# One scan instruction for two states, and lane X's second half moved ahead of scan and exponentials

## The chip, the cores and the metric

The kernel runs on one core of a Trainium2 chip. The core has five instruction streams: TensorE (PE, matmuls; PEld is its weight load), VectorE (DVE), ScalarE (ACT), GpSimd (POOL) and SyncE (SP), which issues nearly all DMA transfers here. Each stream runs in its own order and waits on semaphores where it needs another stream's result. The metric is the device time of one execution in microseconds, and lower is better.

## The reference

The input is `x` of shape (4, 128, 64, 64): 4 images of 128 channels and 4096 pixels. The layers are:

```
x = x + conv_mamba(group_norm(x))          # layer 0
t = tokens(x)                              # (4, 4096, 128)
t = t + attention(layer_norm(t))           # 4 heads of 32, 4096 x 4096 scores
t = t + top2_experts(layer_norm(t))        # 8 experts
```

Inside layer 0 the normalised image goes through a 3x3 depthwise convolution and is cut into four groups of 32 channels. For each group a state-space recurrence runs over the 4096 pixels, with 64 inner channels and 16 states for each of them:

```
dA  = exp(delta * A)               # per inner channel, state, pixel
dBu = delta * B * xin
h   = dA * h + dBu                 # one step per pixel, 16 states side by side
y   = sum over states of h * C
```

`delta`, `B` and `C` depend on the pixel. `B` and `C` are shared by all the inner channels of a group. After that come a gate, a projection, a norm and another projection.

## The kernel before

The pixels of an image are cut into 8 blocks of 512 columns. Two groups of channels with 64 inner channels each fill the 128 partitions, so a block has two parts (`p`) and each part has 16 states (`n`). A *unit* is one state of one part of one block: 4 images x 8 blocks x 2 parts x 16 states = 1024 units. The main loop (line 1244) takes one unit per pass, and a pass is called a *slot*. For its unit a slot issues:

- on SP, one 512 KB load `rows` with `B` and `C` of one state, for the unit three slots later (`fetched`, line 732);
- on ACT, the exponential `da` for the unit two slots later (`decayed`), and a copy of the last column of the previous unit's `h` into `state`, which the next block of the image starts from (line 1253);
- on DVE, three instructions (`scan`, line 747): `h = B * du`, the scan `h`, and `hc = h * C`;
- on PE one slot later, the sum over states: `hc` is added into the PSUM tile `y`. In the first 128 slots (`ALONE`) this is a matmul with the identity. Later it is four transposes of 128 columns (`turned_on`), whose sum is copied to `yT` on ACT after the part's last state and is transposed back a slot later (`turned_back`). DVE then forms `xin` from `y`. There is one `y` buffer.

In the same slot one *group* of attention work is issued (line 1257). A group has two tiles of 128 keys: four score matmuls `sc` on PE, two exponentials `pT` of 128x1024 on ACT, and in the next slot eight products with the values, `av`, on PE (`weighted`). All images together have 1024 groups. Attention for an image starts when its first three blocks are finished, so it lags behind the recurrence and goes on after the last unit. `sc` has two PSUM buffers, so the scores of a slot need the exponentials of the slot before.

All other work is written as generators that stop at each `yield`, and runs in two lanes. Lane Y holds the norms, the convolution and the `inputs` of the recurrence. Lane X holds `closed` (what follows the recurrence up to queries, keys and values) and `finished` (what follows attention, with the experts). `advance(lane, second)` runs one stage. A lane takes one stage in its first half and one in its second half of a slot. A task starts in a first half and ends in one. In lane X all PE work stands in first halves, at the end of a slot, and nearly all DVE and ACT work, which reads its results, stands in second halves.

Nothing reorders this: `Queue` (line 439) chains every instruction of an engine to the one issued before it, so the order of the Python calls is the order of every engine's queue. In a slot that order is:

```
sends; rows load; state copy; da; sc and pT; h, scan, hc; X second half; Y first half;
turned_back; y; Y second half; av; X first half
```

All recorded instructions of the main loop carry line 445, that of the `Queue` helper, so the profile's groups are told apart by their tiles.

## Time and profile before

| | |
|---|---|
| median of 3 runs | 5479.84 us (5469.26 to 5483.6) |
| the profiled execution | 5476.1 us, its span 5474.3 us |
| mean granted TensorE clock | 0.96 |
| PE busy | 4898.3 us (89% of the span) |
| DVE busy | 4126.6 us (75%) |
| ACT busy | 3928.8 us (72%) |
| POOL busy | 1249.9 us (23%) |
| DMA | 1131.83 MB, mean 207 GB/s |

The span starts with the first instruction and ends with the last one. A group of the profile is one kind of instruction on one set of tiles: its row gives the count, the busy time, the mean length of one, and how long its engine had stood idle just before, with what ended that idle time. `out<-in` names the tile written and the tiles read. A median beside a mean shows whether the mean is made by a few long ones. PE's own waits are the best sign of what holds it, since PE is the busiest engine. The table of windows gives each engine's busy time in a stretch of the span.

### The profile page before, as it was taken

The numbers are of one execution on the slowest core, as the hardware profiler recorded it, in microseconds if no ns is written. First come the engines' busy times: TensorE is split into PE (matmuls) and PEld (weight loads), VectorE is DVE, ScalarE is ACT, GpSimd is POOL, SyncE is SP. The second block draws the span as 40 slices with busy tenths as digits, with TensorE's granted clock in tenths as the row PEclk, the third lists the DMA queues.
The fourth block names the chain that finished last, engine by engine and source line by source line (L and its number), as shares of the span: only waits on it lengthen the run. The fifth ranks groups of instructions, "written<-read, shape, count | busy, mean of one in ns | idle before, by whom it ended". The sixth has DMA issues, their size and how long they took to land.

```text
span 5474.3 us, 66026 instructions
## 1 busy us (share of the span) xinstructions
PE 4898.3 (89%) x20778; PEld 2337.6 (43%) x20778; DVE 4126.6 (75%) x6659; ACT 3928.8 (72%) x6045; POOL 1249.9 (23%) x1085
## 2 busy tenths in 40 slices
PE   4677898999999998999999998999999999999997
PEld 2223344444444444444444444444444444444443
DVE  4988778888778888888888888888888888761231
ACT  3555677888777787787877787777777777765553
POOL 2222223223312223223312213222221222200100
PEclk8778999999999999999999999999999999999998
DMA  3556567667666667666766666667766666655442
GB/s 97 175 176 197 190 204 242 224 225 245 218 208 209 222 215 245 221 219 225 257 211 213 213 222 227 231 199 243 253 203 207 205 227 216 234 198 170 166 148 69
DMA packets 451719, 1131.83 MB, mean 207 GB/s; under 512 B 51985, under 2 KB 135330, under 8 KB 451362
## 3 DMA queue, kind: packets, MB, share of 16 engines
q1 hardware_dynamic: 450194, 1126.74, 61.3%
q8 instruction: 167, 2.74, 0.2%
q14 instruction: 190, 1.56, 0.1%
q10 hardware_dynamic: 1168, 0.80, 0.1%
HBM read 967.12 MB, written 143.39 MB: 203 GB/s over the span
## 4 chain that ended last, share of the span: by engine, by line
PE 54%; DVE 19%; ACT 12%; DMA 7%; issue 6%; SPq 1%; POOL 0%; DVEq 0%; ACTq 0%; POOLq 0%
PE av L445 20%; PE sc L445 13%; PE ps_X L445 9%; DVE h L445 9%; PE ps_Y L445 6%; PE y L445 5%; ACT pT L445 4%; ACT xt L445 3%; DMA ks<-kd 2%; ACT L445 2%; DVE hc L445 2%; DMA rows<-bcd 1%; DMA inv<-inverse 1%; DVE share L445 1%; DVE cm L445 1%
## 5 line engine op out<-in xcount | busy, mean ns | idle before, releaser
L445 ACT ACTIVATE pT<-sc 128x1024 f32<-128x1024 f32 x2048 | 1983.7, 1022 | 965.4 <-PE sc L445 962.5
L445 PE MATMUL av<-pT,v 128*64 128x512 f32 x8192 | 1996.9, 608 | 3.8 <-ACT avs L445 3.6
L445 PE MATMUL sc<-qs,ks 128*128 128x512 f32 x4096 | 1302.9, 439 | 99.3 <-DMA ks<-kd 51.4
L445 DVE TENSOR_TENSOR_SCAN h<-da,state,h 128x512 f32<-128x512 f32 x896 | 1240.7, 1385 | 108.5 <-ACT da L445 14.8
L445 PEld LDWEIGHTS sc<-qs,ks 128*128 128x128 f32 x4096 | 715.1, 192 | 773.2 <-ACT pT L445 236.4
L445 DVE TENSOR_TENSOR h<-rows,du 128x512 f32<-128x512 f32 x1024 | 826.3, 807 | 75.1 <-ACT state L445 38.0
L445 DVE TENSOR_TENSOR hc<-rows,h 128x512 f32<-128x512 f32 x1024 | 826.2, 807 | 51.5 <-PE sc L445 0.5
L445 PEld LDWEIGHTS av<-pT,v 128*64 128x64 f32 x8192 | 499.9, 137 | 813.1 <-issue 784.8
L445 ACT ACTIVATE da<-delta,amat 128x512 f32<-128x512 f32 x1024 | 750.5, 733 | 11.1 <-DVE h L445 7.0
L445 PE MATMUL y<-ident,hc 128*128 128x128 f32 x3584 | 555.8, 279 | 57.2 <-DVE xin L445 46.9
L445 PEld LDWEIGHTS y<-ident,hc 128*128 128x128 f32 x3584 | 443.0, 143 | 242.3 <-issue 90.4
L445 ACT ACT_TABLE_LOAD x319 | 409.3, 1283 | 19.3 <-PE ps_Y L445 14.1
L445 POOL TENSOR_TENSOR rsX<-rsX,mhalf 128x4 f32<-128x4 f32 x92 | 114.2, 1241 | 1031.9 <-DVE shiftX L445 1031.9
L445 POOL TENSOR_TENSOR rsY<-rsY,mhalf 128x4 f32<-128x4 f32 x100 | 141.0, 1410 | 826.3 <-DVE shiftY L445 825.5
L445 ACT COPY state<-h 128x1 f32<-128x1 f32 x896 | 176.7, 197 | 191.2 <-DVE h L445 190.7
L445 POOL TENSOR_TENSOR zs<-xin,zs 128x512 f32<-128x512 f32 x64 | 107.4, 1678 | 871.2 <-DVE xin L445 871.2
L445 POOL TENSOR_TENSOR avs<-avs,prev 128x512 f32<-128x512 f32 x96 | 139.3, 1451 | 719.0 <-ACT avs L445 402.7
L445 POOL TENSOR_SCALAR du<-e 128x512 f32<-128x512 f32 x64 | 126.2, 1972 | 578.7 <-ACT e L445 578.7
L445 DVE TENSOR_TENSOR share<-share,xf 128x1024 f32<-128x1024 f32 x128 | 172.6, 1348 | 109.6 <-DMA share<-sharesX 75.3
L445 PE MATMUL ps_X<-share,w_ew 128*128 128x512 f32 x432 | 215.6, 622 | 23.2 <-DVE share L445 23.2
L445 PE MATMUL y<-hc,ident 128*128 128x512 f32 x256 | 169.1, 758 | 42.4 <-DVE hc L445 42.2
L445 DVE TENSOR_TENSOR res<-res,ps_X 128x512 f32<-128x512 f32 x108 | 73.9, 685 | 154.4 <-PE ps_X L445 153.6
(238 smaller groups left out, 4566.2 us busy)
## 6 DMA issues: line engine op xcount, KB each, us to landing
rows<-bcd SPq DMA_DIRECT2D x1024, 512.0 KB
ks<-kd SPq DMA_DIRECT2D x192, 512.0 KB
qs<-qd SPq DMA_DIRECT2D x161, 512.0 KB
share<-sharesX SPq DMA_DIRECT2D x108, 512.0 KB
v<-vd SPq DMA_DIRECT2D x192, 256.0 KB
ks<-kd SPq DMA_DIRECT2D x128, 256.0 KB
avd<-avs SPq DMA_DIRECT2D x96, 256.0 KB
prev<-avd SPq DMA_DIRECT2D x96, 256.0 KB
```

What stands on the lines that cost most here:

```text
L445: return lambda *args, **kw: queued(op(*args, **kw))
```

## The change

A unit now covers two neighbouring states, `n` and `n + 1`, and takes two slots, so the number of slots for the recurrence stays 1024.

- **Layout.** A `rows` load now brings `B` of both states or `C` of both states. It is still 1024 values for each of the 128 partitions, and there is still one load per slot. The host orders the weight `wbc` so that the stored `B` and `C` lie this way.
- **DVE.** In the even slot one multiply of 1024 columns forms both `h` inputs (`driven`), and one scan runs over 1025 columns. Between the two states lies a column whose `da` is zero and whose input is the second state's starting value, so the scan restarts there. In the odd slot one multiply of 1024 columns forms both `hc` (`read`).
- **ACT.** `da` is written one state per slot into one of two fixed tiles, for the next unit. A copy puts the second state's starting value into its column (`carried`). One copy per unit keeps the last columns of both states (`kept`), at the end of the even slot.
- **Order.** Lane X's second half is issued ahead of the attention group and the scan. In the even slot it stands behind `driven`; in the odd slot it stands ahead of `read`. The exponentials are split from the score matmuls (`exponentials`) and follow lane X's second half.
- **Sum over states.** The transposes (`turned_on`, `turned_back`) are used from the start. The two terms are due one and two slots after the odd slot. The first term of a part is due one slot later than that after the first half image (`late`).
- **Buffers.** `h` has 2 of 1026 columns (3 of 512 before), `hc` has 2 of 1024 (5 of 512 before), lane X's `tmp` has 6 (4 before), and `hi` and `lo` of the queries and keys now come from it.

The loop's new text and the helpers are below. The rest of `closed` and the host's ordering of `wbc` are left out.

```diff
--- before.py
+++ after.py
@@ -488,7 +488,9 @@
         return ps_work.tile(shape or [P, BLK], F32, tag=f"work{lane}", name=f"ps_{lane}")
 
     def tmp(lane, name, shape=None):
-        return side.tile(shape or [P, BLK], F32, tag=f"tmp{lane}", name=name, bufs=4)
+        return side.tile(
+            shape or [P, BLK], F32, tag=f"tmp{lane}", name=name, bufs=6 if lane == "X" else 4
+        )
 
     def transposed(lane, src):
         ps = work(lane)
@@ -703,8 +705,8 @@
         held.clear()
         bc = tmp("Y", "bc")[0:DI, :]
         scalar.copy(bc, pb[0:DI, :])
-        bcd = dram.tile([2, NST, 2 * BLK], F32, name="bcd", bufs=4)
-        send(bcd.rearrange("c n (k q) -> (c n k) q", k=2), bc)
+        bcd = dram.tile([2, NST // 2, 2, 2 * BLK], F32, name="bcd", bufs=4)
+        send(bcd.rearrange("c n k (m q) -> (c n k m) q", m=2), bc)
 
         e = tmp("Y", "e")
         scalar.activation(e, ps, AF.Abs, bias=dtb)
@@ -728,34 +730,58 @@
         yield
 
     states = [mix.tile([P, 2, NST], F32, name=f"state{k}") for k in range(2)]
-
-    def fetched(b, i, p, n):
-
-        bcd = in_of[b, i, p][4]
+    decays = [mix.tile([P, 2, BLK + 1], F32, name=f"da{k}") for k in range(2)]
+    for k in range(2):
+        gpsimd.memset(decays[k][:, 0, BLK:], 0.0)
+
+    def fetched(unit, k):
+
+        b, i, p, n = unit
         w = mix.tile([P, 2, BLK], F32, name="rows", bufs=4)
         sync.dma_start(
-            out=w.rearrange("p k q -> p (k q)"),
-            in_=bcd[:, n, :][None].to_broadcast([DI, 2, 2 * BLK]),
+            out=w.rearrange("p m q -> p (m q)"),
+            in_=in_of[b, i, p][4][:, n // 2, k, :][None].to_broadcast([DI, 2, 2 * BLK]),
         )
         return w
 
-    def decayed(b, i, p, n):
-        da = mix.tile([P, BLK], F32, name="da", bufs=3)
-        scalar.activation(da, in_of[b, i, p][2], AF.Exp, scale=amat[:, n : n + 1])
-        return da
-
-    def scan(b, i, p, n, w, da):
-
+    def decayed(unit, da, k):
+        b, i, p, n = unit
+        scalar.activation(
+            da[:, k, 0:BLK], in_of[b, i, p][2], AF.Exp, scale=amat[:, n + k : n + k + 1]
+        )
+
+    def carried(unit):
+
+        b, i, p, n = unit
+        if (i, p, n) == (0, 0, 0):
+            gpsimd.memset(states[b % 2], 0.0)
+        h = mix.tile([P, 2, BLK + 1], F32, name="h", bufs=2)
+        scalar.copy(h[:, 0, BLK:], states[b % 2][:, p, n + 1 : n + 2])
+        return h
+
+    def kept(unit, h):
+        b, i, p, n = unit
+        if i < NB - 1:
+            scalar.copy(states[b % 2][:, p, n : n + 2], h[:, :, BLK - 1])
+
+    def driven(unit, h, w):
+        b, i, p, n = unit
         du = in_of[b, i, p][3]
-        h = mix.tile([P, BLK], F32, name="h", bufs=3)
-        vector.tensor_mul(h, w[:, 0, :], du)
+        vector.tensor_mul(h[:, :, 0:BLK], w, du[:, None, :].to_broadcast([P, 2, BLK]))
+
+    def scan(unit, h, da):
+
+        b, i, p, n = unit
+        h, da = (a.rearrange("p k q -> p (k q)")[:, 0 : 2 * BLK + 1] for a in (h, da))
         vector.tensor_tensor_scan(
-            out=h, data0=da, data1=h, initial=0.0 if i == 0 else states[b % 2][:, p, n : n + 1],
+            out=h, data0=da, data1=h, initial=states[b % 2][:, p, n : n + 1],
             op0=ALU.mult, op1=ALU.add,
         )
-        hc = mix.tile([P, BLK], F32, name="hc", bufs=5)
-        vector.tensor_mul(hc, w[:, 1, :], h)
-        return h, hc
+
+    def read(h, w):
+        hc = mix.tile([P, 2, BLK], F32, name="hc", bufs=2)
+        vector.tensor_mul(hc, w, h[:, :, 0:BLK])
+        return hc
 
     def scanned(b, i, p, y):
         xin, zs, delta, du, bcd = in_of.pop((b, i, p))
...
@@ -961,7 +983,7 @@
                     nxt = parts[at + 1]
                     if ready(b, nxt):
                         ahead = load(nxt, qs if nxt[:2] == (q, h) and not nxt[5] else None)
-                pTs = []
+                scs = []
                 for j in range(g, g + STEP):
                     sc = ps_sc.tile([P, 2, BLK], F32, name="sc")
                     for u in range(2):
@@ -969,14 +991,20 @@
                             sc[:, u, :], ks[:, j * P : (j + 1) * P],
                             qs[:, u * BLK : (u + 1) * BLK],
                         )
-                    pT = att.tile([P, 2, BLK], F32, name="pT", bufs=4)
-                    scalar.activation(pT, sc, AF.Exp, scale=ATT_SCALE)
-                    pTs.append((v[:, j // NT, j % NT, :], pT))
+                    scs.append((v[:, j // NT, j % NT, :], sc))
                 yield (
-                    b, q, h, pTs, first and g == 0, last and g + STEP == NT * n, prev, final,
+                    b, q, h, scs, first and g == 0, last and g + STEP == NT * n, prev, final,
                 )
 
     sums, partial, total, inverse, later = [None], {}, {}, {}, deque()
+
+    def exponentials(group):
+        pTs = []
+        for v, sc in group[3]:
+            pT = att.tile([P, 2, BLK], F32, name="pT", bufs=4)
+            scalar.activation(pT, sc, AF.Exp, scale=ATT_SCALE)
+            pTs.append((v, pT))
+        return *group[:3], pTs, *group[4:]
 
     def weighted(group):
         b, q, h, pTs, first, last, prev, final = group
@@ -1162,12 +1190,12 @@
         while True:
             if lane not in running:
 
-                tasks = lanes[lane] if lanes[lane] or slot < len(units) else lanes["X"]
+                tasks = lanes[lane] if lanes[lane] or slot < END else lanes["X"]
                 if not tasks or not all(k in done for k in tasks[0][2]):
                     return False
 
                 if (
-                    tasks[0][0][0] == "out" and slot < len(units) + 4
+                    tasks[0][0][0] == "out" and slot < END + 4
                     and not 2 <= slot % (2 * NST) < NST + 2
                 ):
                     return False
@@ -1236,53 +1264,70 @@
         left.clear()
 
     groups = attention_groups()
-    units = [(b, i, p, n) for b, i in blocks for p in range(2) for n in range(NST)]
-
-    ALONE = NB // 2 * 2 * NST
-    rows, decays, old, due, closing = {}, {}, None, deque(), deque()
-    y_of, waiting, slot = {}, None, 0
-    while slot < len(units) or due or closing or waiting or left or later or lanes["X"] or running:
+    units = [(b, i, p, n) for b, i in blocks for p in range(2) for n in range(0, NST, 2)]
+    END = 2 * len(units)
+
+    ALONE = NB // 2 * NST
+    rows, due, closing, y_of = {}, deque(), deque(), {}
+    h_of, slot = {}, 0
+
+    def fetch(*wanted):
+        for ahead, k in wanted:
+            if ahead < len(units):
+                until(("in", *units[ahead][:3]))
+                rows[ahead, k] = fetched(units[ahead], k)
+
+    def prepared(ahead, k):
+        if ahead < len(units):
+            decayed(units[ahead], decays[ahead % 2], k)
+            if k:
+                h_of[ahead] = carried(units[ahead])
+
+    def ends(unit):
+        return unit[3] == NST - 2
+
+    waiting = None
+
+    while slot < END or due or closing or waiting or left or later or lanes["X"] or running:
+        at, odd = divmod(slot, 2)
         flush()
-
-        for ahead in range(slot if slot == 0 else slot + 3, min(slot + 4, len(units))):
-            until(("in", *units[ahead][:3]))
-            rows[ahead] = fetched(*units[ahead])
-        if old:
-            (b, i, p, n), h = old
-            if i < NB - 1:
-                scalar.copy(states[b % 2][:, p, n : n + 1], h[:, BLK - 1 : BLK])
-            old = None
-        for ahead in range(slot if slot == 0 else slot + 2, min(slot + 3, len(units))):
-            decays[ahead] = decayed(*units[ahead])
+        if slot == 0:
+            fetch((0, 0), (0, 1), (1, 0))
+            prepared(0, 0)
+            prepared(0, 1)
+        fetch((at + 2, 0) if odd else (at + 1, 1))
+        unit = units[at] if at < len(units) else None
+        prepared(at + 1, odd)
+        if unit and not odd:
+            h = h_of.pop(at)
+            driven(unit, h, rows.pop((at, 0)))
+        advance("X", True)
         group = next(groups, None)
-        if slot < len(units):
-            unit = units[slot]
-            h, hc = scan(*unit, rows.pop(slot), decays.pop(slot))
-            old = unit, h
-            b, i, p, n = unit
-
-            due.append((slot + 1, unit, hc, n == 0))
-        advance("X", True)
+        if group:
+            group = exponentials(group)
+        if unit and not odd:
+            scan(unit, h, decays[at % 2])
+        if unit and odd:
+            hc = read(h, rows.pop((at, 1)))
+            late = slot >= ALONE and unit[3] == 0
+            due.append((slot + 1 + late, unit, 0, hc[:, 0, :], False))
+            due.append((slot + 2, unit, 1, hc[:, 1, :], ends(unit)))
         advance("Y", False)
         while closing and closing[0][0] <= slot:
             turned_back(*closing.popleft()[1:])
         while due and due[0][0] <= slot:
-            at, unit, term, first = due.popleft()
-            b, i, p, n = unit
+            _, (b, i, p, n), k, term, done_with = due.popleft()
+            first = n == 0 and k == 0
             if first:
                 y_of[b, i, p] = ps_y.tile([P, BLK], F32, name="y")
-            y, ends = y_of[b, i, p], n == NST - 1
-            if at <= ALONE:
-                mm(y, ident, term, first, ends)
-                if ends:
-                    summed_up(b, i, p, y_of.pop((b, i, p)))
-            else:
-                turned_on(y, term, first, ends)
-                if ends:
-                    yT = mix.tile([P, BLK], F32, name="yT")
-                    scalar.copy(yT, y_of.pop((b, i, p)))
-                    closing.append((slot + 1, b, i, p, yT))
+            turned_on(y_of[b, i, p], term, first, done_with)
+            if done_with:
+                yT = mix.tile([P, BLK], F32, name="yT")
+                scalar.copy(yT, y_of.pop((b, i, p)))
+                closing.append((slot + 1, b, i, p, yT))
         advance("Y", True)
+        if unit and not odd:
+            kept(unit, h)
         if waiting:
             weighted(waiting)
         waiting = group
...
```

More of the change, by code (lines that the diff above doesn't have):

```diff
@@ L852, in closed @@
             yield
-            hi = side.tile([P, BLK], F32R, name="hi", bufs=2)
-            vector.tensor_scalar(hi, ps, bias, None, ALU.add)
-            lo = side.tile([P, BLK], F32R, name="lo", bufs=2)
-            vector.scalar_tensor_tensor(
-                lo, ps, bias, hi.bitcast(F32), ALU.add, ALU.subtract
-            )
+            hi, lo = tmp("X", "hi"), tmp("X", "lo")
+            vector.tensor_scalar(hi.bitcast(F32R), ps, bias, None, ALU.add)
+            vector.scalar_tensor_tensor(lo.bitcast(F32R), ps, bias, hi, ALU.add, ALU.subtract)
             for half, w in enumerate((hi, lo)):
-                w = w.bitcast(F32)
                 if len(d.shape) == 4:
@@ L1338, in _laid_out @@
     wout = np.zeros((P, 2, P), np.float32)
-    wbc = np.zeros((P, 2, NST, 2), np.float32)
+    wbc = np.zeros((P, 2, NST // 2, 2, 2), np.float32)
     xdt, dtT = np.zeros((4, P), np.float32), np.zeros((4, P), np.float32)
@@ L1347, in _laid_out @@
             wout[d, p, s] = c0["out_proj_w"].T
-        wbc[d, c] = c0["x_proj_w"][2:].reshape(2, NST, DI).transpose(2, 1, 0)
+        wbc[d, c] = c0["x_proj_w"][2:].reshape(2, NST // 2, 2, DI).transpose(3, 1, 0, 2)
         xdt[2 * c : 2 * c + 2, d] = c0["x_proj_w"][:2]
```

## The prediction

> **What bounds it now.** I read the page's busy rows and slices first, then the windows, then PE's own waits by stretch, then the groups, and last the order of time around single waits.
>
> ```profile
> PE 4898.3 (89%) x20778; PEld 2337.6 (43%) x20778; DVE 4126.6 (75%) x6659; ACT 3928.8 (72%) x6045; POOL 1249.9 (23%) x1085
> ...
> PE   4677898999999998999999998999999999999997
> ...
> DVE  4988778888778888888888888888888888761231
> ...
> PEclk8778999999999999999999999999999999999998
> ```
>
> The slices show three stages. Up to about 684 us DVE is the fuller engine, PE is not, and its clock is low. Up to 4790 us PE is above 90% and DVE near 80%. After that only PE is full.
>
> ```profile
> 137.00:274.00 137.00, 90.62 (x187) 34.65 (x185) 124.82 (x187) 68.60 (x135) 36.65 (x31) 0.76 0.51 174
> 274.00:411.00 137.00, 99.22 (x230) 40.17 (x231) 120.89 (x183) 71.76 (x137) 35.02 (x31) 0.77 0.53 176
> ...
> 2463.00:2600.00 137.00, 125.83 (x570) 61.40 (x567) 114.25 (x185) 108.55 (x173) 42.34 (x35) 1.00 0.67 226
> ```
>
> The columns are length, then PE, PEld, DVE, ACT and POOL busy, clock, DMA share, GB/s. Early, DVE is busy 125 and 121 of 137 us. In the middle PE is busy 126 of 137. Over 684 to 4790 us the windows sum to 3787 us of PE in 4106 us, so PE stands still for 319 us. That is all that a change which leaves PE's work alone can win there. PE's waits in that stretch:
>
> ```profile
> PE y L445 <- DVE xin L445: 45.2, 53, 1.5
> PE sc L445 <- ACT pT L445: 44.5, 69, 3.0
> PE ps_X L445 <- DVE aT L445: 43.0, 20, 4.2
> PE sc L445 <- DMA ks<-kd: 33.8, 13, 5.1
> PE ps_X L445 <- ACT xt L445: 33.5, 39, 5.8
> PE ps_X L445 <- DVE prX L445: 33.2, 17, 2.9
> PE ps_X L445 <- DVE share L445: 23.2, 20, 2.6
> PE ps_X L445 <- DVE lo L445: 13.6, 8, 3.5
> ```
>
> The columns are total us, times, longest. Five rows (`aT`, `xt`, `prX`, `share`, `lo`, 146.5 us) are one thing: PE waits for lane X's second half. One such wait in order of time:
>
> ```profile
> 2529.38 1.60 DVE L445 TENSOR_TENSOR hc<-rows,h 128x512 f32<-128x512 f32 x1
> ...
> 2530.90 0.68 DVE L445 TENSOR_TENSOR res<-res,ps_X 128x512 f32<-128x512 f32 x1
> ...
> 2531.50 1.70 DVE L445 TENSOR_TENSOR share<-share,xf 128x1024 f32<-128x1024 f32 x1
> ...
> 2533.25 1.98 PE L445 MATMUL ps_X<-share,w_ew 128*128 128x512 f32 x4 [1.22 <-DVE share L445]
> ```
>
> `res` and `share` stand behind `hc` in DVE's queue, and PE pays 1.22 us for it.
>
> **Part 1, fewer and longer DVE instructions.** The groups, with mean length; the medians, from the view by tile, are 684 ns (`h` multiply), 1284 (scan), 692 (`hc`) and 1219 (`share`):
>
> ```profile
> L445 DVE TENSOR_TENSOR_SCAN h<-da,state,h 128x512 f32<-128x512 f32 x896 | 1240.7, 1385 | 108.5 <-ACT da L445 14.8 <-DVE h L445 2.7 <-ACT pT L445 0.5
> L445 DVE TENSOR_TENSOR h<-rows,du 128x512 f32<-128x512 f32 x1024 | 826.3, 807 | 75.1 <-ACT state L445 38.0 <-POOL du L445 25.7 <-DMA rows<-bcd 11.4
> L445 DVE TENSOR_TENSOR hc<-rows,h 128x512 f32<-128x512 f32 x1024 | 826.2, 807 | 51.5 <-PE sc L445 0.5 <-DVE h L445 0.5
> ```
>
> `share` is the nearest row for the 1024-column multiplies: same operation, same broadcast. From 684 and 1219 a column costs 1.045 ns and an instruction 0.149 us. No row shows a 1025-column scan. If all but 0.149 us grows with the columns it takes 0.149 + 1.135 x 1025/512 = 2.42 us; if the 59 ns that a start value adds (1284 against a median of 1225 without) are fixed too, 2.36; twice the old one is 2.57. I take 2.42. A pair of states then goes from 2 x (0.684 + 1.284 + 0.692) = 5.32 us to 1.219 + 2.42 + 1.219 = 4.86, a saving of 0.46 us, or 236 us over 512 pairs.
>
> The means give more: 6.00 against 5.20 us, so 0.80 us a pair, 410 us. Here a rule decides. Rows reach 1.78 us where the median is 0.69, and in the trace those stand beside POOL instructions. The Trainium skill ("SBUF — State Buffer", section on the two separate sides) says that VectorE with two SBUF inputs and GpSimd take a shared port pair as an exclusive lock for a whole instruction. So the excess is paid per POOL instruction, whose number does not change, and 0.46 holds. It also speaks against the change: POOL can now stand behind 2.42 us instead of 1.28. The norm's power on POOL has an idle stage before `xt` reads it (ACT waits 7.9 us for `shiftX` in the whole middle), which hides 1.1 us.
>
> What DVE's saving is worth depends on the stage. *Early*: 152 units ran by 684 us, so 76 x 0.46 = 35 us if DVE always set the pace. It is 88% busy (361 of 410 us in 137 to 547 us), and the chain there also runs over PE, ACT and issue. I take two thirds, **-23 us** (bounds 0 and -61, by the mean). *Middle*: nothing by itself; DVE has a fifth of its time free.
>
> **Part 2, the order.** Lane X has no PE work in second halves, so PE's order hardly changes. The second halves issue no DMA (their sends are queued for later slots), and their POOL instructions already stood ahead of lane Y's, so SP's and POOL's orders stay. What changes is what DVE and ACT do first. The chain shows a slot of plain work as `sc` 1.14, `y` 0.44 and `av` 1.87 us: PE gives lane X's second half 3.45 us of cover. On DVE 2.66 us of scan work stood ahead of it, and afterwards 1.22 (even) or nothing (odd):
>
> - `share`: 2.66 + 0.69 + 1.22 = 4.57, so 1.1 us late (the row: 23.2/20 = 1.16). Afterwards 3.1, not late.
> - `prX`: about 17 small instructions, 3.4 us in order of time. Afterwards late by 1.2 in even slots only.
> - `lo`: 2.66 + 1.5 = 4.2, afterwards 2.7.
> - `xt` on ACT: 0.57 for the first score, 1.94 of `pT`, then 1.5, so 0.6 late. Afterwards `xt` runs while the scores do, and `pT` starts about 1 us later. ACT waits 696 us for `sc` in this stretch, which covers it. Without that cover it would cost that 1 us in each of about 90 norms.
> - `aT`: 2.66 + 0.69 is within 3.45, yet PE waited 2.15 us each time. DVE was late for other reasons, so I leave most of it.
>
> Left over I reckon 30 (`aT`), 10, 3, 3 and 5 us, so 95 us go. Where lane Y's POOL bursts make DVE the limit over several slots, order does not help, so I take **-80 us** (bounds 0 and -146).
>
> What is now behind it: the scan, then `kept` on ACT, and behind that the next `da`, lane X's ACT work and `pT`. `da` is also only one slot ahead instead of two. With 1.9 us of lane X work and 2.42 of scan, `kept` falls near 4.5 us after the slot's first score, and the next-but-one scores need its `pT` at about 7. The 64 extra ACT copies (960 of 0.2 us for 896) vanish in the same idle time. I put new waits at **+20 us** (bounds 0 and what the slower rival below costs).
>
> **Part 3, sum over states.** `y <- xin` is PE waiting because the next part's first term needs the single `y` buffer in the slot in which DVE still reads it. `late` moves that term one slot on: **-43 us** of 45. `y <- hc` (6.7 us) goes too, **-5**. Early, transposes take the place of matmuls: 144.4/214 x 2 = 1.35 us a unit against 0.62 (555.8/896), or about 1.1 at the lowest clock. It counts only for some 20 early attention slots that PE fills: **-10 us**. Against it, the skill ("TensorE: Matmul & The Clock Gate", part 4) says that transposes do not count as activity that releases the full clock. If so, the early clock falls from 0.77 to 0.5: PE's work other than `y` and attention is some 8% of that stretch's chain, 34 us, which grows by half, +19. By the trace, where transposes run at 0.99, it is nothing, but attention runs beside them there. I take **+10**. The early sums come two slots later, and attention with them: 2 x 3.7 = **+7 us**.
>
> **Sum.** Early -23 - 10 + 10 + 7 = -16. Middle -80 - 43 - 5 + 20 = -108. Tail: the same rows after 4790 us hold little, -6. Together -130 us. The profiled execution took 5476.1 us (span 5474.3), 3.7 below the median, too little to shift: **5346 us**.
>
> **Rivals.**
> - *Everything gives way* (0.14). DVE reaches lane X's work so early that `aT` goes as well and the page's mean is the true DVE saving: 319 - 120 = 199 in the middle, 45 early, 6 late, so 5226 us. For it: PE's chain share is only 54%. Against it: `ks` (33.8) and `pT` (44.5), the latter from ACT's table loads, are untouched.
> - *The waits only move* (0.14). PE comes earlier to the next late thing in lane Y, or a double-length DVE instruction costs as much as two. Only `xin` and the early transposes are won: 5476 - 43 - 10 + 17 = 5440 us, spread 5415 to 5490.
> - *Slower* (0.12): the scan behind lane X. In each even slot DVE first waits for PE's first-half result, then works 1.9 to 3.4 us for lane X, then scans for 2.42, and ACT stands at `kept` with `pT` behind it. 425 even slots lie in the middle, so 0.3 us each eats the whole 130 us. At 0.5 us it is 5476 - 130 + 213 = 5559 us. For it: ACT already waited 190.7 us for `h`. Against it: only 54.4 us of that in the middle, and `pT` has most of a slot to spare.
>
> **How the numbers follow.** The likeliest case has 0.60 and a range of its own from 5290 to 5400. Measurement tells about 0.3%, 16 us. Faster by more: 0.60 + 0.14 + 0.09 of the moving waits = 0.83; the same 0.05; slower 0.12. The range 5215 to 5465 leaves out the slower case, the top of the moving waits and the bottom of the first rival, together 0.2.
>
> **What would show it.** Right: the two 1024-column multiplies near 1.22 us and the scan near 2.4 by median; DVE busy some 240 us less; PE's waits for `xin` near zero and for `share`, `prX`, `lo`, `xt` down to a third; PE idle in the middle near 210 us. Wrong: ACT's wait `state <- h` grown past 150 us, with `sc <- pT` grown too; an early clock near 0.5; or DVE's saving nearer 400.

## The result and the profile after

The changed kernel takes **5385.1 us** (median; 5380.7 to 5388.3) against 5478.8 us for the kernel before on the same chip (5469.3 to 5483.6). The ratio is 0.9831, 95% interval 0.9814 to 0.9848: 94 us faster, where 130 were forecast. The profiled execution has a span of 5378.9 us, before 5474.3.

One correction to the description of the change above: `late` starts at slot 64 (`ALONE` is now `NB // 2 * NST`), so from the third block of the first image on, not after half an image.

The page's busy rows and slices of the changed kernel, the same rows as were shown of the kernel before:

```profile
PE 4850.0 (90%) x21066; PEld 2366.3 (44%) x21066; DVE 3757.2 (70%) x5123; ACT 3926.8 (73%) x6117; POOL 1525.0 (28%) x1091
...
PE   4556898999999999999999999999999999999997
...
DVE  4888767777777778877778778777777877751332
...
PEclk7677899999999999999999999999999999999998
```

DVE lost 369 us, more than the 236 forecast, and POOL gained 275 us, which no step of the forecast had. The clock of the second to fourth slice fell from 7, 7, 8 to 6, 7, 7. The windows (length; PE, PEld, DVE, ACT, POOL busy; clock; DMA share; GB/s):

```profile
137.00:274.00 137.00, 74.56 (x278) 45.56 (x276) 114.63 (x131) 63.84 (x131) 46.80 (x30) 0.70 0.53 175
274.00:411.00 137.00, 82.46 (x326) 50.31 (x326) 114.93 (x132) 78.51 (x151) 47.52 (x32) 0.74 0.55 182
2463.00:2600.00 137.00, 128.54 (x558) 60.99 (x555) 104.40 (x113) 109.53 (x170) 52.35 (x33) 0.99 0.75 261
```

PE's waits in the middle, 700 to 4650 us (total us, times, longest):

```profile
PE sc L445 <- ACT pT L445: 73.2, 155, 3.0
PE ps_Y L445 <- ACT xt L445: 36.2, 44, 1.3
PE sc L445 <- DMA ks<-kd: 32.0, 14, 3.8
PE ps_X L445 <- DVE aT L445: 23.9, 16, 3.4
PE av L445 <- ACT avs L445: 15.7, 23, 1.6
PE ps_X L445 <- ACT xt L445: 13.4, 14, 3.0
...
PE ps_X L445 <- DVE lo L445: 4.1, 2, 3.3
```

In the same stretch the kernel before had 43.5 us for `xin`, which is gone, and 145.4 for the five rows of lane X's second half (`aT` 42.7, `prX` 33.2, `xt` 32.7, `share` 23.2, `lo` 13.6), of which 41 is left. But `pT` rose from 39.8 to 73.2, lane Y's `xt` from 11.6 to 36.2, and `avs` from 1.8 to 15.7: 72 us of new waits.

The trace also gives the time by stage. The marks are the start of DVE's `hc` for state 128 and for state 1022, counted through all 1024:

| kernel | to state 128 | 128 to 1022 | PE idle in it | after 1022 |
|---|---|---|---|---|
| before | 580 | 4299 | 343 | 595 |
| changed | 568 | 4222 | 251 | 589 |

So early -12 us, middle -77, tail -6, where -16, -108 and -6 were forecast. In the middle the waits fell by 92 us, but PE's busy time grew by 15.

### The profile page after: what moved, and what is told of

Its sections match the earlier page's. It is cut to its first block, busy times and chain, and to the rows that moved or that the text cites. A ratio compares the mean times of both kernels' runs of the same rounds, so it can differ in the third digit from the quotient of the medians.

```text
span 5378.9 us, 64061 instructions
## 1 busy us (share of the span) xinstructions
PE 4850.0 (90%) x21066; PEld 2366.3 (44%) x21066; DVE 3757.2 (70%) x5123; ACT 3926.8 (73%) x6117; POOL 1525.0 (28%) x1091
## 5 line engine op out<-in xcount | busy, mean ns | idle before, releaser
L445 ACT ACTIVATE pT<-sc 128x1024 f32<-128x1024 f32 x2048 | 1985.7, 1024 | 637.2 <-PE sc L445 635.5
L445 PE MATMUL av<-pT,v 128*64 128x512 f32 x8192 | 2011.1, 612 | 16.7 <-ACT avs L445 16.4
L445 DVE TENSOR_TENSOR_SCAN h<-da,state,h 128x1025 f32<-128x1025 f32 x512 | 1275.5, 2491 | 198.2 <-ACT h L445 168.9
L445 DVE TENSOR_TENSOR h<-rows,du 128x1024 f32<-128x1024 f32 x512 | 707.8, 1382 | 53.0 <-POOL du L445 28.5
L445 DVE TENSOR_TENSOR hc<-rows,h 128x1024 f32<-128x1024 f32 x512 | 700.9, 1369 | 18.2 <-PE y L445 4.4
L445 PE MATMUL y<-ident,hc 128*128 128x128 f32 x4096 | 639.5, 285 | 64.3 <-DVE hc L445 56.9
L445 PEld LDWEIGHTS y<-ident,hc 128*128 128x128 f32 x4096 | 523.5, 147 | 269.2 <-issue 116.7
L445 POOL TENSOR_TENSOR rsX<-rsX,mhalf 128x4 f32<-128x4 f32 x92 | 232.7, 2530 | 843.1 <-DVE shiftX L445 843.1
L445 POOL TENSOR_TENSOR rsY<-rsY,mhalf 128x4 f32<-128x4 f32 x100 | 171.5, 1715 | 795.7 <-DVE shiftY L445 795.7
L445 ACT COPY state<-h 128x2 f32<-128x2 f32 x448 | 87.8, 196 | 416.3 <-DVE h L445 412.4
L445 ACT ACTIVATE xt<-ps_Y,shiftY,rsY 128x128 f32<-128x128 f32 x380 | 143.0, 466 | 67.9 <-POOL shiftY L445 60.7
```

The costliest lines, as they stand in the source:

```text
L445: return lambda *args, **kw: queued(op(*args, **kw))
```

## The experiments

### The order undone, and the order alone

```diff
         driven(unit, h, rows.pop((at, 0)))
-        advance("X", True)
         group = next(groups, None)
...
+        advance("X", True)
         advance("Y", False)
```

> The changed kernel with lane X's second half put back behind the exponentials and the scan or read; everything else stays. Theory A (the order wins the middle stage): PE's waits for share, prX, lo, aT and xt of lane X, which fell from about 145 to 42 us between 700 and 4650 us, come back to over 100 us, while the new waits (pT, avs) shrink a little; the time is 5440 to 5470 us. Rival B (fewer DVE instructions win it, by leaving DVE free earlier): those waits stay below 70 us and the time is at most 5405 us.

Measured: **5366.2 us**, ratio 0.9799 (0.9783 to 0.9816). Without the new order the changed kernel is 19 us *faster*. The two intervals just touch; the stage marks, further down, show the difference more clearly. PE's waits in the middle with the old order:

```profile
PE sc L445 <- ACT pT L445: 42.3, 66, 3.0
...
PE ps_X L445 <- DVE aT L445: 36.0, 17, 5.3
PE ps_X L445 <- ACT xt L445: 32.2, 40, 5.8
PE ps_X L445 <- DVE lo L445: 17.5, 26, 4.8
PE ps_Y L445 <- ACT xt L445: 15.2, 22, 0.9
PE ps_X L445 <- DVE share L445: 6.5, 7, 2.6
PE ps_X L445 <- DVE prX L445: 5.4, 17, 1.0
PE av L445 <- ACT avs L445: 4.8, 13, 0.7
```

`share` and `prX` are nearly gone here too, so the order isn't what removed them. What the order takes from `aT`, `xt` and `lo` it puts into `pT`, lane Y's `xt` and `avs`.

The other way round, the kernel before with only its order changed (exponentials and the three DVE instructions behind lane X's second half):

```diff
+        advance("X", True)
         group = next(groups, None)
+        if group:
+            group = exponentials(group)
         if slot < len(units):
...
-        advance("X", True)
```

> The kernel before, one state a slot, with lane X's second half put ahead of the exponentials and of the three DVE instructions. Theory A: PE's waits for share, prX and lo go, xin stays at 45 us, and the time is 5400 to 5430 us. Rival B: 5460 us or more.

Measured: **5547.3 us**, ratio 1.0134 (1.0117 to 1.0151), 68 us slower. PE's largest waits in its middle:

```profile
PE y L445 <- DVE hc L445: 122.0, 139, 3.6
PE y L445 <- DVE xin L445: 47.9, 50, 2.4
```

With one state a slot, `hc` is due in the next slot. Behind lane X it comes late, and the row forecast to fall, `hc`, becomes the largest. The rows of lane X's second half do fall there, to 17 us together (`aT` 12.2, `lo` 2.6, `prX` 2.3, `xt` 0.3), so the order does what it was meant for, and loses more at `hc`.

### Which half of the order costs

The second half of lane X moved back behind the exponentials alone (ACT's old order, DVE's new one):

```diff
-        advance("X", True)
         group = next(groups, None)
         if group:
             group = exponentials(group)
+        advance("X", True)
```

> The changed kernel with lane X's second half behind the exponentials on ACT, but still ahead of the scan or read on DVE: half of the order undone. Theory C (on ACT the new order costs, on DVE it pays): PE's wait for pT falls from 82 to about 48 us and lane Y's xt with it, lo, share and prX stay near zero, and the time is 5330 to 5355 us, below the 5366 of the kernel with the whole order undone. Theory D (on DVE it costs, since the scan and POOL's rsX behind it come later): the time is 5378 to 5400 us.

Measured: 5377.1 us, 0.9814 (0.9798 to 0.983). And ahead of the exponentials but behind scan and `read`:

```diff
-        advance("X", True)
         group = next(groups, None)
-        if group:
-            group = exponentials(group)
...
+        advance("X", True)
+        if group:
+            group = exponentials(group)
         advance("Y", False)
```

> The other half undone: lane X's second half behind the scan or read on DVE, but ahead of the exponentials on ACT. Theory C: the cost on ACT stays without the gain on DVE, so PE's wait for pT stays near 80 us and the time is 5395 to 5425 us. Theory D: rsX on POOL is short again (1.4 us against 2.5), xt comes in time, and the time is 5340 to 5370 us.

Measured: 5371.2 us, 0.9803 (0.9787 to 0.9819). Each lies between the two whole orders, and their intervals overlap with both, so the times don't divide the 19 us. The waits do, in part. With DVE's order alone `pT` is back at 42.5 and lane Y's `xt` at 14.2, but `avs` stays at 16.9, and lane X's `xt` is 63.2. With the whole old order `xt` stood behind the exponentials too and cost 32.2; POOL's norm power `rsX`, which it needs, took 1.03 us by median there and takes 3.06 here, as in the changed kernel, where the 53 longest of 92 all run beside a scan. Whether that makes `xt` late was not shown (see the kernel with lane X ahead of all DVE work, below). With ACT's order alone lane Y's `xt` is 32.7, `pT` 56.0 and `avs` 5.2. So lane Y's `xt` comes from ACT doing lane X's work before the exponentials, and so does about half of the growth of `pT`; `avs` comes from DVE's order, and the rest of `pT` only when both are changed.

### ACT's wait for the scan

The forecast's slower case had ACT standing at `kept`, and in the changed kernel ACT does wait 412.4 us for it over the whole span (190.7 before). `kept` moved to the odd slot, behind the exponentials:

```diff
+        if unit and odd:
+            kept(unit, h)
...
-        if unit and not odd:
-            kept(unit, h)
```

> The changed kernel with the copy of the two states' last columns moved from the end of the even slot to the odd slot, behind its exponentials. Theory A (ACT standing at this copy for the long scan makes the exponentials and lane Y's xt late): ACT's wait of 412 us for h falls below 100, PE's waits for pT (82 us) and for lane Y's xt (87 us) fall by half, and the time is 5335 to 5360 us. Rival B (xt is late because POOL stands behind the longer DVE instructions): ACT's wait falls, PE's waits for xt stay, and the time is within 10 us of 5385.

Measured: 5383.1 us, 0.9833 (0.9817 to 0.9849): no difference. ACT's wait for the scan fell to 88 us, and PE's waits stayed (`pT` 71.0 in the middle). The line of the changed kernel:

```profile
ACT state L445 <- DVE h L445: 412.4, 157, 7.9
```

ACT spends the time it gets back waiting for something else: 792.0 us for the scores (635.5 before the move) and 152.3 for `shiftX` of lane X's norm (38.0). The wait of 412 us cost nothing that these runs can tell.

### The later first term

```diff
-            late = slot >= ALONE and unit[3] == 0
+            late = 0
```

> The changed kernel with the first term of a part due one slot after its odd slot always. Theory A (the xin wait was PE's own time): y waits for xin 50 times or more again, 40 us in all, and the time is 5420 to 5430 us. Rival B (PE only waits there for what it would wait for a moment later): the wait returns and the time stays within 10 us of 5385.

Measured: **5460.3 us**, 0.9969 (0.9959 to 0.9979). Without `late` the changed kernel loses 75 of its 94 us. The `xin` row is back (43.7 us in the middle, 51 times). The marks put 45 of the 75 us down to PE standing still between states 128 and 1022 (296 us for 251), and 31 to PE being slower there (busy 4002 us for 3971), which the last section of the experiments comes to. The same in the kernel before, and nothing else:

```diff
-            due.append((slot + 1, unit, hc, n == 0))
+            late = slot >= ALONE and n == 0
+            due.append((slot + 1 + late, unit, hc, n == 0))
```

> The kernel before with one thing of the change: the first term of a part is due one slot later, from slot 128 on. Theory A (the wait for xin is PE's own time whatever else is done): the wait of 45 us goes and the time is 5425 to 5440 us. Theory E (the late term is needed only because the long scan delays xin, so it pays less here than the 75 us it pays in the changed kernel, and PE would wait anyway): 5460 to 5480 us.

Measured: **5430.4 us**, 0.991 (0.9893 to 0.9927): 48 us, with a forecast of 43. In the middle PE is idle for 299 us instead of 343, and the other rows stay: `aT` 41.8, `prX` 32.8, `share` 20.4.

### What is the rest: fewer instructions, or where they stand

From 5430 (`late` alone) to 5366 (everything but the order) are 64 us. First the two-state instructions of the 5366 kernel were cut in two again, in the same places:

```diff
-        vector.tensor_mul(h[:, :, 0:BLK], w, du[:, None, :].to_broadcast([P, 2, BLK]))
+        for k in range(2):
+            vector.tensor_mul(h[:, k, 0:BLK], w[:, k, :], du)
...
+        for k in range(2):
+            vector.tensor_tensor_scan(
+                out=h[:, k, 0:BLK], data0=da[:, k, 0:BLK], data1=h[:, k, 0:BLK], ...
...
-        vector.tensor_mul(hc, w, h[:, :, 0:BLK])
+        for k in range(2):
+            vector.tensor_mul(hc[:, k, :], w[:, k, :], h[:, k, 0:BLK])
```

> The changed kernel with the order of before (lane X's second half behind the exponentials and the scan), and every two-state DVE instruction cut in two: two multiplies and two scans of 512 columns in the even slot, two multiplies in the odd slot. Only the DVE instructions' number and length differ from the run with the order back (5366 us). Theory F (fewer instructions take DVE's time off lane X's path): DVE is busy 4090 to 4130 us again, PE's waits for prX, share and lo rise to 60 us or more, and the time is 5410 to 5435 us, that of the kernel before with the late term. Rival G (what counts is that the odd slot puts little DVE work ahead of lane X): DVE is as busy, the waits stay below 45 us and the time is 5360 to 5385 us.

Measured: **5360.7 us**, 0.9787 (0.9771 to 0.9804), so no slower than with the long ones:

```profile
PE 4822.5 (90%) x21066; PEld 2358.2 (44%) x21066; DVE 3944.2 (74%) x6659; ACT 3925.7 (73%) x6117; POOL 1323.6 (25%) x1091
```

DVE has its 6659 instructions of before again and 178 us more work than the 3766.6 of the uncut kernel, POOL 165 us less (1323.6 for 1488.9), and no time is lost. But the cut also changes a wait: each scan now takes its start value from `state` itself, and DVE no longer waits for ACT's copy into `h` (`carried`). DVE's waits for ACT in the middle, first of the uncut kernel, then of this one:

```profile
DVE h L445 <- ACT h L445: 190.4, 106, 8.8
```

```profile
DVE h L445 <- ACT da L445: 89.0, 58, 7.3
```

The uncut kernel with that copy and `da` issued earlier takes 5341.9 us (below). So these runs don't show what fewer instructions alone are worth; up to 19 us (5360.7 - 5341.9) can be theirs, and they are not the 64.

Then the same instructions were put back where they stood before, one state to each slot:

```diff
-        if unit and not odd:
-            scan(unit, h, decays[at % 2])
-        if unit and odd:
-            hc = read(h, rows.pop((at, 1)))
...
+        if unit:
+            scan(unit, h, decays[at % 2], odd)
+            hc = read(h, wc, odd)
+            late = slot >= ALONE and unit[3] == 0 and not odd
+            due.append((slot + 1 + late, unit, odd, hc, bool(odd) and ends(unit)))
```

(`driven` takes one state too, `kept` moves to the odd slot, `hc` has three single buffers and `rows` and `share` keep theirs, with a fifth.)

> Base: the changed kernel with lane X's second half back behind the exponentials and with every two-state instruction of VectorE cut in two (5360.7 us, 0.9787). Only the place of those instructions changes here: each slot gets one state (multiply, scan, multiply, so 2.7 us of VectorE work ahead of lane X in every slot, as in the kernel before) in place of 4.0 us in the even slot and 1.4 us in the odd one; a state's sum then comes in the next slot, and the copy of the states in the odd slot. Theory L (the uneven pattern is what is left of the gain, because lane X is free early in every odd slot): the 64 us between the kernel before with the later first term alone (5430) and the changed kernel with the old order (5366) come back, so 5410 to 5435 us, ratio 0.988 to 0.992, and TensorE again waits 20 us or more each for share and prX in the middle. Rival M (the layout of the rows, the transposes from the start and the deeper buffers of lane X carry it): 5350 to 5375 us, ratio 0.977 to 0.981, with share and prX below 10 us each. In between, both have a part.

Measured: **5417.0 us**, 0.9893 (0.9876 to 0.9909). 56 us are lost again, and so the place of the instructions is the cause, with what moves along with it: a state's sum is due one slot after it, and `kept` comes in the odd slot. Neither looks large: PE waits 5.3 us for `hc` in the middle, and the move of `kept` was worth nothing above. PE's waits in its middle:

```profile
PE ps_X L445 <- DVE aT L445: 43.3, 17, 4.1
...
PE ps_X L445 <- DVE prX L445: 32.9, 17, 2.9
...
PE ps_X L445 <- DVE share L445: 19.8, 20, 1.5
```

These are the rows of the kernel before. In the two-slot pattern four DVE instructions, 3.9 us by their medians, stand in the even slot and two, 1.4 us, in the odd one; in the one-slot pattern each has 2.7. In an odd slot lane X then comes 1.3 us earlier, without a change of order. Even slots have it 1.3 us later, and yet the five rows of lane X's second half come to 100 us in the two-slot pattern and to 141 with one state a slot. That this is because of the odd slots is argued; no run moved the instructions of one kind of slot alone.

### The early stage

Identity matmuls for the first four blocks, as before the change, in place of transposes:

```diff
+            if (b, i) < (0, 4):
+                mm(y_of[b, i, p], ident, term, first, done_with)
+                if done_with:
+                    summed_up(b, i, p, y_of.pop((b, i, p)))
+                continue
             turned_on(y_of[b, i, p], term, first, done_with)
```

> The changed kernel with the sum over states of the first four blocks (128 slots) done by matmuls with the identity, and without transposing back, as before. If transposes keep the clock down, the granted clock between 137 and 411 us rises from 0.72 to 0.77 or more and the time falls by 5 to 15 us (5370 to 5380). If only the number of instructions matters, PE has more to do in the early attention slots and the time rises by 5 to 15 us (5390 to 5400).

Measured: 5391.5 us, 0.9842 (0.9826 to 0.9859), 6 us above the changed kernel with overlapping intervals, so not clearly different. The first of the two early windows:

```profile
137.00:274.00 137.00, 86.31 (x198) 35.45 (x197) 114.76 (x133) 68.98 (x139) 46.81 (x31) 0.80 0.54 179
```

The clock is 0.80 and 0.79 for 0.70 and 0.74, and state 128 comes at 570 us for 568. So the clock is lower with the transposes, where PE is also less busy (74.56 us for 86.31 in the first window). The run gives back both the shorter work and the lower clock: together they are worth nothing here, and what each is worth by itself it does not tell.

### A version that is faster

In the 5366 kernel DVE waits 190 us in the middle for ACT's copy into `h` (`carried`), which the changed kernel issues only one slot ahead. Both ACT steps one slot earlier:

```diff
             prepared(0, 1)
+            prepared(1, 0)
...
-        prepared(at + 1, odd)
+        prepared(at + 2 if odd else at + 1, 1 - odd)
```

> The changed kernel with the order of before (5366 us), and da and the copy of the second state's start issued one slot earlier, as far ahead of the scan as before. Theory J (DVE's wait of 247 us for that copy makes lane X late): the wait falls below 80 us, PE's waits for aT and lo fall, and the time is 5335 to 5355 us. Rival K (DVE waits there because it has run ahead, and nothing is late): the wait falls and the time is within 8 us of 5366.

Measured: **5341.9 us**, 0.9753 (0.9737 to 0.9769), the fastest of all. DVE's waits for that copy between 137 and 570 us, first of the 5366 kernel, then of this one:

```profile
DVE h L445 <- ACT h L445: 33.9, 12, 6.9
```

```profile
DVE h L445 <- ACT h L445: 12.7, 4, 4.8
```

State 128 comes at 564 us for 578, the middle takes 4180 for 4185. So of the 20 us by the two profiles 14 lie early, where DVE is the fuller engine, and the 190 us in the middle had cost 6. The split is less sure than the sum, since the changed kernel, with the same late copy, reached state 128 at 568.

Then lane X was moved ahead of *all* DVE work of the slot, in the kernel with DVE's order alone (5377.1 us):

```diff
         h = h_of.pop(at)
-            driven(unit, h, rows.pop((at, 0)))
...
         advance("X", True)
         if unit and not odd:
+            driven(unit, h, rows.pop((at, 0)))
             scan(unit, h, decays[at % 2])
```

> The changed kernel with lane X's second half behind the exponentials on ACT (5377 us so) and now ahead of all three DVE instructions, so that after it comes a multiply and not the scan. Theory H (POOL's rsX stands behind the scan that follows it, 2.53 us, and makes lane X's xt late): rsX falls to 2.0 us or less on the mean, PE's wait for lane X's xt falls from 63 to below 45 us, and the time is 5350 to 5368 us. Rival I (xt is late because DVE itself comes late to the second half, or because the scan and with it the copy on ACT come later still): the time is 5372 to 5400 us.

Measured: **5460.6 us**, 0.9973 (0.9963 to 0.9984), 84 us slower than its base. PE's largest waits in its middle:

```profile
PE ps_X L445 <- ACT xt L445: 89.2, 65, 4.3
...
PE av L445 <- ACT avs L445: 35.2, 35, 2.8
...
PE ps_X L445 <- DVE share L445: 24.2, 14, 1.9
```

DVE now stands idle until PE's first-half result is there: `cm <- ps_X` 149.0 us for 93.4, `hi <- ps_X` 93.1 for 67.0. The 1.2 us of `driven` had filled that time; now it comes behind lane X, and so does the scan. The idea behind this run was that `rsX` on POOL, beside the scan, makes lane X's `xt` late: `rsX` did fall, from 2.53 to 1.92 us by mean, and the wait for `xt` rose from 63.2 to 89.2 all the same. Being first in a queue is worth nothing while the input is not there.

### Where the order's 19 us went

The same stage marks for the kernels above, ordered so that each row adds to the row before it, with a count from the trace: `av` matmuls between the marks that took over 900 ns, where the median is 592 and the maximum 1117, so about half speed.

| kernel | median | to 128 | 128 to 1022 | PE idle in it | long `av` | in groups |
|---|---|---|---|---|---|---|
| before | 5478.8 | 580 | 4299 | 343 | 48 | 10 |
| `late` alone | 5430.4 | 579 | 4253 | 299 | 56 | 13 |
| + layout, transposes, buffers; one state a slot | 5417.0 | 576 | 4240 | 291 | 34 | 8 |
| + two-slot pattern, instructions cut | 5360.7 | 568 | 4186 | 247 | 31 | 9 |
| + two-state instructions | 5366.2 | 578 | 4185 | 248 | 30 | 8 |
| + lane X ahead (the changed kernel) | 5385.1 | 568 | 4222 | 251 | 112 | 28 |

The order adds 37 us in the middle, and only 3 of them are waits (in these two executions it wins 10 before state 128 and 5 after 1022). The other 34 are PE being busy for longer with the same instructions: there are 82 more `av` near half speed, which take 473 ns more than the median by mean. `av` overlap (8192 of 612 ns are 2011.1 us busy, so 2.5 at a time), which makes 16 us of it; `av` is 2011 of PE's 4850 us, so over all PE work it comes to an estimated 38 us, near the 34. The granted clock agrees: by the mean of four runs each it is 0.951 in the changed kernel and 0.957 with the old order, and 0.006 of 5379 us is an estimated 32 us. All kernels with lane X ahead of the exponentials have more long `av` than those with the old order, which have 30 to 56: 160 without `late`, 120 with `kept` later, 110 with early matmuls, 75 with ACT's order alone, 90 in the kernel before with the order. With DVE's order alone it is 62, and 90 with lane X ahead of all DVE work. Of the 28 groups, 15 begin just after a wait of 0.65 to 1.15 us for lane Y's `xt`; with the old order none does. Such a wait is not enough: between the marks there are 42 for that `xt` of 0.6 us or more in the changed kernel, and 19 with the old order. One of the 15, PE in order of time in the changed kernel (start, length):

```profile
1666.07 0.73 PE L445 MATMUL sc<-qs,ks 128*128 128x512 f32 x2 [0.57 <-ACT pT L445]
1666.97 0.73 PE L445 MATMUL sc<-qs,ks 128*128 128x512 f32 x2 [0.17 <-ACT pT L445]
1668.85 1.12 PE L445 MATMUL ps_Y<-ident,xt 128*128 128x128 f32 x4 [1.14 <-ACT xt L445]
1669.76 1.06 PE L445 MATMUL y<-ident,yT 128*128 128x128 f32 x4
1670.75 2.64 PE L445 MATMUL av<-pT,v 128*64 128x512 f32 x8
```

and two windows of 3.41 us there (columns as above; the clock is the third number from the end):

```profile
1665.38:1668.79 3.41, 1.58 (x5) 0.59 (x4) 2.71 (x2) 3.41 (x8) 0.34 (x2) 1.00 0.71 211
1668.79:1672.20 3.41, 3.35 (x12) 2.10 (x14) 0.75 (x1) 3.39 (x6) 0.52 (x1) 0.50 0.45 141
```

The clock is at half from 1668.79 us on, so it had fallen before the four transposes `ps_Y` began: these were slowed by it (1.12 us, where four took 0.71 at 1664.78) and did not bring it down. In the 3.41 us before, PE was busy for 1.58, nearly all of it with four `sc`, and stood still for the rest, in three waits. In this trace the clock changes in steps of 3.41 us. From 700 to 4700 us it falls 38 times in the changed kernel and 21 times with the old order. In the step before, PE was busy with other work than transposes for less than 45% in 37 of the 38 cases, and in 19 of the 1083 steps at full clock that no fall followed. With the transposes counted as work, 22 of the 38 are below 45%.

The Trainium skill ("TensorE: Matmul & The Clock Gate", part 1) has the clock return to half after an idle window of about 3.4 us. The length of the step is seen here, but PE need not be idle for all of it: in the step above it worked for 46% of the time, and the clock fell. Part 4 has transposes not counted as busy. The counts above lean that way, but it does not hold in full. In the early stage of the changed kernel one such step holds twelve transposes and 0.2 us of other work, and the clock rises after it:

```profile
153.27:156.68 3.41, 3.02 (x13) 2.23 (x11) 3.05 (x10) 1.26 (x5) 0.00 (x0) 0.50 0.08 34
156.68:160.09 3.41, 0.66 (x4) 0.42 (x4) 3.31 (x4) 0.86 (x2) 3.08 (x2) 1.00 0.59 204
```

All this is counted from traces; no run changed such a place alone. That the half-speed stretches come with the order is shown by the counts of eight kernels with it, whole or in part, against those without.

## Why the prediction was right and wrong

**Direction and size.** Faster was right; 94 us in place of 130 is within the likeliest case's own range only at its upper end (5385 of 5290 to 5400), and half of the reasons were wrong. That the sum came so near is in part luck: the order's -80 did not come, and 56 us from the two-slot pattern, which it had not foreseen, stood in their place. Of its three signs of being wrong two came, ACT's wait for the scan past 150 us with `pT` grown, and a DVE saving near 400 us (369).

**Part 2, the order (-80): wrong.** The slot arithmetic itself held. The five rows of lane X's second half fell by 104 us (95 forecast). But 48 of these go without any change of order (145.4 to 97.6 in the kernel with the old one), and the forecast didn't see where from: the two-slot pattern, which it wrote down only as fewer and longer instructions, leaves one multiply of 1.2 us in odd slots. The order brings the other 56, and pays for them. The step that failed is "ACT waits 696 us for `sc` in this stretch, which covers it". The later exponentials were not covered: `pT`, lane Y's `xt` and, from DVE's side, `avs` grew by 63 us against the old order (72 against before), where **+20** were set down for all new waits. Then PE ran 34 us slower in the middle, a term the sum didn't have. So the order is worth +19, not -80. A rival had "the waits only move" at 5440; for the order that is what happened, at the price of the clock besides.

**New waits at `kept` (+20, with the slower rival behind it): wrong place.** ACT's wait for the scan grew past 150 us as that rival said (412.4), and moving it away won nothing.

**Part 3, `late` (-43): right, and too small.** -48 alone, `xin` gone from the waits; in the changed kernel it carries 75, of which 45 are waits and 31 PE's speed. `hc` (-5) went as said, 6.7 to 1.3.

**Part 1, DVE's saving: durations right, rule applied to the wrong side.** The groups and POOL's norm power in the changed kernel:

```profile
L445 DVE TENSOR_TENSOR_SCAN h<-da,state,h 128x1025 f32<-128x1025 f32 x512 | 1275.5, 2491 | 198.2 <-ACT h L445 168.9 <-ACT pT L445 0.5
L445 DVE TENSOR_TENSOR h<-rows,du 128x1024 f32<-128x1024 f32 x512 | 707.8, 1382 | 53.0 <-POOL du L445 28.5 <-DMA rows<-bcd 24.5
L445 DVE TENSOR_TENSOR hc<-rows,h 128x1024 f32<-128x1024 f32 x512 | 700.9, 1369 | 18.2 <-PE y L445 4.4
...
L445 POOL TENSOR_TENSOR rsX<-rsX,mhalf x92: 1006/3055/3077, 45.2 to 5333.6; 128x4 f32<-128x4 f32 x92
```

The medians by tile are 1220 ns for the multiplies (1.219 forecast) and 2354 for the scan (2.42 taken, 2.36 as the other bound). By medians a pair saves 0.53 us, by means 0.76 (6.00 to 5.24): the end that the forecast rejected, 0.80, was nearer. From the exclusive lock in the Trainium skill's "SBUF — State Buffer", section on the two separate sides, it had inferred that DVE's excess is paid per POOL instruction and stays. The sums fit such a lock, but with long DVE instructions more of the excess falls on POOL: in the same order POOL is busy 1488.9 us with the long ones and 1323.6 with the cut ones. `rsX` is another matter: with the long instructions and the old order its median is still 1.03 us, and 3.06 comes with the order, which puts it beside a scan that keeps its 2.35. DVE plus POOL were 5377 us and are 5282, so about three quarters of DVE's gain is time that moved to POOL. What DVE's saving is worth in time stays open: cut in two again the kernel is as fast, but then DVE does not wait for `carried` either, so at most 19 us.

**Early (-16 forecast, -12 measured): about right as a sum; its terms were not measured singly.** The work's -10 and the clock's +10 cancel by the run with matmuls, as forecast. The lower clock is seen (0.77 to about 0.72), but not by the rule it was put down to: a step with almost nothing but transposes brought the clock to full. The forecast said "an early clock near 0.5" would prove it wrong; it stayed well above. The early stage still lost time to a wait that the forecast named in half a sentence ("`da` is also only one slot ahead"): taking it away wins 24 us, most of it early by the stage marks.

**Tail (-6): right.**

## What to carry to other kernels

When two orders are compared, count what comes *later* on every engine with the same care as what comes sooner, and look for the cover of the delayed work at that place in the slot, not in a sum over the stage: ACT's 696 us of waiting did not cover 1 us in the right place. Merging instructions changes two things, their number and the pattern of work over time; cut them again in place to see which one pays, and look whether the cut changes a wait as well. A big wait is a candidate, not a cost: 412 us at `kept` over the whole span were worth nothing, and 190 us at `carried` in the middle 6 us, while a 44 us row (`xin`) was worth 48 to 75. And a wait can cost twice, while PE stands still and where PE is slower after it: without `late` the changed kernel lost 45 and 31 us so.

## What was not expected of the hardware

- PE need not be idle for the clock to fall: after a step of 3.41 us in which products other than transposes filled less than 45%, it was at half in the next one in 37 of 56 cases (changed kernel, 700 to 4700 us). There are 38 falls in the changed kernel for 21 with the old order, 34 us in 4222, though PE is 94% busy there. And a step with almost nothing but twelve transposes, busy for 3.02 us of it, brought it back to full.
- The excess time that DVE and POOL share moves with the length of the DVE instruction. The same work, cut or not: DVE 3944.2 and POOL 1323.6, or 3766.6 and 1488.9; the sums, 5268 and 5255, hardly differ. A 128x4 operation on POOL took 3.06 us beside a 1025-column scan, and 1.03 where the order kept it away from one.
- Where the instructions stand matters as well: the same 6659 DVE instructions take 3944.2 us in the two-slot pattern and 4122.8 with one state a slot, POOL 1323.6 and 1268.3.
- A scan over 1025 columns takes 2354 ns, 1.83 times one over 512 (1284).
